# The end block of a key band and the short chunk of w_down as half-array products, one behind the other

## The chip, the core and the metric

The kernel runs on one core of a Trainium2 chip. The metric is the device time of one execution in microseconds (us), as a median over runs. Five engines share the work: TensorE (matrix products; PE in the profile, its weight loads are PEld), VectorE (DVE), ScalarE (ACT), GpSimd (POOL), and SyncE (SP), which issues most DMAs. A product of TensorE has a stationary operand, which is loaded first, and a moving operand, whose columns are streamed past it. Both have the contraction on the 128 partitions. The sum goes to PSUM, in banks.

## The reference

One transformer block with two halves, on X of 8 sequences, 2048 positions and 256 features, all in float32:

```
def layer(x):
    x = x + attention(layernorm(x))
    return x + ffn(layernorm(x))

def attention(X):                       # D[n, m] = 0.9 ** |n - m|
    Q, K, V = xpos(X @ W_Q), xpos(X @ W_K, downscale=True), X @ W_V
    p = softmax(Q @ K.T) * D            # the decay comes after the softmax
    return p @ V

def ffn(x):                             # fq: blocks of 16 along the last axis,
    gate = fq(x) @ fq(w_gate).T         # rounded to 4-bit floats and scaled back
    y = fq(x) @ fq(w_up).T              # w_gate, w_up: (704, 256)
    return fq(silu(gate) * y) @ fq(w_down).T    # w_down: (256, 704)
```

All scores are needed for the softmax's maximum and sum. In the product with V, however, a key that is 833 positions away has the weight 0.9^833, about 8e-39, which is below float32's normal range.

## The kernel before, in words

The 16,384 positions are 128 blocks of 128 rows, numbered n; i = n % 16 is a block's place in its sequence. The program is written by hand in its order, step by step: `step(n)` (from L842) emits the work of a software pipeline on all five engines. For block n it computes the scores (`scores`, two halves of 1024 keys), their maxima (`maximum`, VectorE, L543) and the exponentials (ScalarE). For block n-1 it does the decays, the product with V, the residual and the second normalization; for n-2 the gate and up products; for n-3 the rounding of the hidden values, mostly on VectorE and GpSimd; for n-5 the down product and the output. Each engine runs its instructions in the order in which they are emitted. Waits are semaphores that are derived from the tiles that an instruction reads and writes. Only the last steps (from `z = total - 1` on) are written out separately.

**The band.** `band(n)` is the list of key blocks from i-7 to i+7 that exist (BAND = 7): 8 blocks at a sequence's ends, up to 14 or 15 in its middle. `turn_p` turns the exponentials so that keys lie on the partitions (transposes on VectorE within 32x32 squares, L261, and a DMA there and back). `decays` (L621) multiplies them by the decay table into the tile p_t, on VectorE, in pieces of up to four blocks in key order. `attend` (L636) then runs one product for each key block, in key order, into the PSUM tile o: p_t's block is stationary, the block of V moving (L644). Within the band's outermost blocks only half the keys are within 833 positions. For the two middle blocks of a sequence (i = 7 and 8, `whole`), whose bands have an outermost block at both ends, `join_values` puts the two useful halves of V into one tile, so that one product does for both ends. All other blocks have one such end: i+7, the last in key order, for i up to 6; i-7, the first, for i from 9 on. It is taken with all 128 partitions.

**The short chunk.** The 704 hidden features are FC = 6 chunks for `down` (L768): 640 are five whole chunks, 64 are left. The sixth chunk takes features 576 to 703, so that it has 128 rows; the first 64 of them were in the fifth chunk already, and the rows of `wd_t` (w_down turned) that they meet are set to zero (L163). `turn_h` (L743) turns h in two pieces, 640 and the last 128 features; `keep_h` copies the result to `h_t`. The six products of `down` go into the PSUM tile d.

**The order around the change.** On TensorE a step is: scores of block n, a projection in most steps, `down(n-5)`, `attend(n-1)`, then gate and up of n-2. On VectorE, between the second maximum and the rounding of h stands `decays(n-1)`.

Every float32 product is a pair of weight loads and a pair of passes in the profile. o and d have PSUM buffers of their own (pool `ps_m`, two buffers).

Of the kernel before, what the change touches and what calls it, by code (L numbers as in the profile page):

```python
# [9 lines left out]
F32 = mybir.dt.float32  # L10
# [5 lines left out]
P = 128  # L16
GROUP = 512
BPG = GROUP // P
# [3 lines left out]
BAND = 7  # L22
SQ = 32
NSQ = P // SQ
# [10 lines left out]
def preln_xpos_retention_fp4_ffn_kernel(  # L35
# [13 lines left out]
    nc = tc.nc  # L49
    B, L, H = x.shape  # L50
    F = w_gate.shape[0]
    HC = H // P
    NB = L // P
    NG = L // GROUP
    FH = F // 2
    FC = -(-F // P)
# [8 lines left out]
    ps_m = ctx.enter_context(tc.tile_pool(name="ps_m", bufs=2, space=bass.MemoryType.PSUM))  # L65
# [58 lines left out]
    ident = cpool.tile([P, P], F32, name="ident")  # L124
# [35 lines left out]
    wg_t = cpool.tile([P, HC, F], F32, name="wg_t")  # L160
    wu_t = cpool.tile([P, HC, F], F32, name="wu_t")
    wd_t = cpool.tile([P, FC, H], F32, name="wd_t")
    nc.gpsimd.memset(wd_t[: FC * P - F, FC - 1, :], 0.0)  # L163


    def layernorm_scale(mv, n, name):
# [82 lines left out]

    def turn(dst, pieces, name, tag):


        n = sum(src.shape[-1] for src in pieces) // NSQ
        sq = prob_p.tile([P, dst.shape[-1]], F32, tag=tag, bufs=1, name=f"sq_{name}")
        sq = sq[:, : NSQ * n].rearrange("p (c f) -> p c f", c=NSQ)
        at = 0
        for src in pieces:
            w = src.shape[-1] // NSQ  # L260
            nc.vector.transpose(  # L261
                sq[:, :, at : at + w].rearrange("p c (k i) -> p k c i", i=SQ),
                src.rearrange("p (k c i) -> p k c i", c=NSQ, i=SQ),
            )
            at += w
        there = dram.tile([NSQ, SQ, NSQ, n], F32, tag=f"turn_{n}", name=f"there_{name}")
        nc.scalar.dma_start(there.rearrange("a i c f -> (a i) c f"), sq)
        dst = dst[:, : NSQ * n].rearrange("p (a f) -> p a f", a=NSQ)
        for c in range(NSQ):
            nc.sync.dma_start(dst[ts(c, SQ)], there[:, :, c, :].rearrange("a i f -> i a f"))  # L270
# [5 lines left out]

    LAST = (FC - 1) * P - (F - P)

# [4 lines left out]
    weight_rows, weight_fp4, scratch = {}, {}, {}  # L287

    def hold_ffn_weights():
        for name in "gu":  # L290
            weight_rows[name] = act_p.tile(
                [P, FULL - 1, H], F32, tag="kt", bufs=2 * NG, name=f"w{name}_rows"
            )
        whole = act_p.tile([P, 2 * GROUP], F32, tag="kt", bufs=2 * NG, name="wgu_rows")
        weight_rows["r"] = whole[:, : 3 * H].rearrange("p (c k) -> p c k", c=3)
        scratch["r"] = whole[:, 3 * H :]
        big = act_p.tile([P, 2 * GROUP], F32, tag="kt", bufs=2 * NG, name="wbig")
        for c in range(HC):
            whole = act_p.tile([P, BPG * H], F32, tag="vt", bufs=6, name=f"wd_rows{c}")
            weight_rows["d", c] = whole[:, :F]  # L300
            scratch["gu"[c]] = whole[:, F:]
        for key in "gur":
            raw = weight_rows[key].rearrange("p c k -> p (c k)")
            weight_fp4[key] = Fp4(raw, P, raw.shape[-1], f"w{key}", big, scratch[key])
        for c in range(HC):
            weight_fp4["d", c] = Fp4(weight_rows["d", c], P, F, f"wd{c}", big)

    def load_ffn_weights(key):
        if key in ("g", "u"):
            src = {"g": w_gate, "u": w_up}[key]  # L310
            nc.sync.dma_start(
                weight_rows[key], src[: (FULL - 1) * P, :].rearrange("(c p) k -> p c k", p=P)
            )
        elif key == "r":
            raw = weight_rows[key]
            for c, src in enumerate((w_gate, w_up)):
                nc.sync.dma_start(raw[:, c, :], src[(FULL - 1) * P : FULL * P, :])
                nc.sync.dma_start(raw[c * REST : (c + 1) * REST, 2, :], src[FULL * P :, :])
        else:
            nc.sync.dma_start(weight_rows[key], w_down[ts(key[1], P), :])  # L320

    def turn_ffn_weights(key):
        raw = weight_rows.pop(key)
        if key[0] == "d":
            cols, per = ts(key[1], P), FC // 2
            for first in range(0, FC, per):
                pt = ps_m.tile([P, per, P], F32, tag="m", name=f"pt_wd_{first}")
                for fc in range(first, first + per):
                    at = min(fc * P, F - P)
                    nc.tensor.transpose(pt[:, fc - first, :], raw[:, at : at + P], ident)  # L330
                whole = min(per, FC - 1 - first)
                nc.scalar.copy(wd_t[:, first : first + whole, cols], pt[:, :whole, :])
                if whole < per:
                    nc.scalar.copy(wd_t[LAST:, FC - 1, cols], pt[LAST:, per - 1, :])
            return
        n = raw.shape[1]
        if key == "r":
            pts = []
            for hc in range(HC):
                pt = ps_m.tile([P, n, P], F32, tag="m", name=f"pt_wr_{hc}")  # L340
                for c in range(n):
                    nc.tensor.transpose(pt[:, c, :], raw[:, c, ts(hc, P)], ident)
                pts.append(pt)
            for c, dst in enumerate((wg_t, wu_t)):
                for hc, pt in enumerate(pts):
                    nc.scalar.copy(dst[:, hc, (FULL - 1) * P : FULL * P], pt[:, c, :])
                    nc.scalar.copy(dst[:, hc, FULL * P :], pt[:, 2, c * REST : (c + 1) * REST])
            return
        pt = ps_s.tile([P, 2 * GROUP], F32, tag="s", name=f"pt_w{key[0]}")
        pt = pt[:, : HC * n * P].rearrange("p (h c r) -> p h c r", h=HC, c=n)  # L350
        for hc in range(HC):
            for c in range(n):
                nc.tensor.transpose(pt[:, hc, c, :], raw[:, c, ts(hc, P)], ident)
        dst = {"g": wg_t, "u": wu_t}[key]
        nc.scalar.copy(dst[:, :, : n * P].rearrange("p h (c r) -> p h c r", c=n), pt)
# [36 lines left out]
    qt, kt, vt = {}, {}, {}  # L392
# [127 lines left out]
    total = B * NB  # L520
# [74 lines left out]
    def band(n):  # L595
        return [k for half in range(2) for k in keys_of(n, half)]
# [3 lines left out]
    ends_of = {}  # L600

    def whole(n):
        return BAND <= n % NB < NB - BAND
# [32 lines left out]
    def attend(n):  # L636
        b, i = divmod(n, NB)
        po = ps_m.tile([P, H], F32, tag="m", name=f"o_{n}")
        keys, p_t = band(n), turned.pop(n)
        values = [(j, vt[b, k // BPG][:, k % BPG, :]) for j, k in enumerate(keys)]  # L640
        if whole(n):
            values = values[1:-1] + [(0, ends_of.pop(n))]
        for j, v in values:
            nc.tensor.matmul(  # L644
                po, p_t[:, j, :], v, start=(j == values[0][0]), stop=(j == values[-1][0])
            )
        attended[n] = po

    def inverse_sum(n):
# [93 lines left out]
    def turn_h(n):  # L743
        h = hid[n][1]
        if n >= total - 4:
            pt = ps_s.tile([P, FC + 2, P], F32, tag="s", name=f"pt_h_{n}")[:, :FC, :]
            at_once = FC // 2 if n == total - 1 else FC
            for f in range(0, FC, at_once):
                for fc in range(f, f + at_once):
                    at = min(fc * P, F - P)  # L750
                    nc.tensor.transpose(pt[:, fc, :], h[:, at : at + P], ident)
                chunks = slice(f, f + at_once)
                keep_h(n, pt.rearrange("p c (a i) -> p c a i", a=NSQ)[:, chunks], chunks)
        else:
            turn(h, [h[:, : (FC - 1) * P], h[:, F - P : F]], f"h{n}", "sq_h")

    def keep_h(n, src=None, chunks=slice(0, FC)):
        x1, h, h_t = hid[n]
        if chunks.start == 0:
            h_t = ffn_p.tile([P, FC, P], F32, tag="h_t", name=f"h_t_{n}")  # L760
        nc.scalar.copy(  # L761
            h_t[:, chunks].rearrange("p c (a i) -> p c a i", a=NSQ),
            in_runs(h) if src is None else src,
        )
        hid[n] = (x1, h, h_t)


    def down(n):  # L768
        x1, _, h_t = hid.pop(n)
        pd = ps_m.tile([P, H], F32, tag="m", name=f"d_{n}")  # L770
        pairs = [(h_t[:, fc, :], wd_t[:, fc, :]) for fc in range(FC)]
        if z - 5 < n < z:
            pairs.insert(0, (ident, x1))
        for j, (lhs, rhs) in enumerate(pairs):
            nc.tensor.matmul(pd, lhs, rhs, start=(j == 0), stop=(j == len(pairs) - 1))  # L775
        hid[n] = (x1, pd)
# [16 lines left out]
    pairs = [range(c, c + 2) for c in range(0, BPG, 2)]  # L793
# [236 lines left out]
    half = FC // 2 * P // QBLK  # L1030
# [60 lines left out]
```

## Time and profile before

| | |
|---|---|
| median of 3 runs | 2833.9 us (2833.09 to 2834.87) |
| the profiled execution's own time | 2833.93 us |
| its span in the profile | 2832.1 us |
| granted clock of TensorE | 0.998 |
| busy: TensorE, loads | 2809.3 us, 1842.3 us |
| busy: VectorE, GpSimd, ScalarE | 2476.0, 1412.8, 1078.0 us |
| a step, in the middle of the run | 19.4 to 23.7 us |

Times in the profile are counted from the span's start. A group's row gives source line, engine, operation, the tiles written and read (out<-in), the form, how often, then the busy time in us and the mean length of one in ns, then the idle time of the engine just before them and who ended it. A row of the timeline gives start and length in us, engine, line, operation, tiles, form and how many instructions were merged into it, with idle time before it in brackets. Matmul records are longer than the distance from one to the next, since they overlap.

### The profile page before, as it was taken

What the parts mean: (1) busy time and instruction counts of PE and PEld (TensorE: products, weight loads), DVE (VectorE), ACT (ScalarE), POOL (GpSimd) and SP (SyncE); (2) the same over time, 40 slices, a digit from 0 to 9 for tenths busy, and PEclk for the clock granted to TensorE, in tenths of its full rate; (3) what the DMA queues carried; (4) which work ended last, traced back from release to release, by engine and by line L of the source; (5) the groups of instructions that cost most, each with busy time, mean ns of one, the idle gap of its engine ahead of it and who ended that gap; (6) DMA issues with size and microseconds to landing.
All of it is one profiled execution on the core that took longest, in us unless ns stands there. A gap on an engine that the chain in (4) does not pass through costs nothing.

```text
span 2832.1 us, 34344 instructions
## 1 busy us (share of the span) xinstructions
PE 2809.3 (99%) x9754; PEld 1842.3 (65%) x9754; DVE 2476.0 (87%) x5665; ACT 1078.0 (38%) x1707; POOL 1412.8 (50%) x1328
## 2 busy tenths in 40 slices
PE   9899999999999999999999999999999999999999
PEld 6566666666666666666666666666666666666666
DVE  8988888988888888898888888888888888888888
ACT  4333334333433443333334333433343343333332
POOL 6554455444555445544555544554545445545443
PEclk9999999999999999999999999999999999999999
DMA  5355544555455555555544555455545554445541
GB/s 192 115 169 171 170 142 147 176 180 155 142 162 170 166 159 155 154 161 171 161 152 152 167 174 161 145 168 167 167 145 160 166 167 148 143 123 160 150 152 50
DMA packets 364320, 441.45 MB, mean 156 GB/s; under 512 B 101600, under 2 KB 311648, under 8 KB 364128
## 3 DMA queue, kind: packets, MB, share of 16 engines
q1 hardware_dynamic: 306096, 263.58, 34.5%
q10 hardware_dynamic: 58032, 175.66, 16.3%
q8 instruction: 77, 1.26, 0.2%
q14 instruction: 115, 0.94, 0.1%
HBM read 246.68 MB, written 192.41 MB: 155 GB/s over the span
## 4 chain that ended last, share of the span: by engine, by line
PE 88%; DVE 5%; POOL 1%; ACT 1%; issue 1%; DMA 1%; SPq 0%; DVEq 0%; ACTq 0%; POOLq 0%
PE s L531 28%; PE o L644 21%; PE d L775 10%; PE gate L710 10%; PE up L710 10%; PE pp_q L467 3%; PE pp_k L467 3%; PE pv L505 3%; DVE m L543 1%; DVE p_t L614 0%; DMA there_p<-sq_p 0%; DVE h L739 0%; DVE amax_h L192 0%; POOL h L239 0%; POOL h L240 0%
## 5 line engine op out<-in xcount | busy, mean ns | idle before, releaser
L531 PE MATMUL s<-kt,qt 128*128 128x512 f32 x2048 | 900.7, 592 | 2.2 <-DVE rot_q L487 2.0
L531 PEld LDWEIGHTS s<-kt,qt 128*128 128x128 f32 x2048 | 388.3, 190 | 459.5 <-issue 420.1
L644 PE MATMUL o<-v,p_t 128*128 128x256 f32 x2880 | 646.6, 381 | 8.1 <-DVE p_t L614 8.1
L644 PEld LDWEIGHTS o<-v,p_t 128*128 128x128 f32 x2880 | 548.2, 191 | 88.2 <-issue 7.6
L564 ACT ACT_TABLE_LOAD x125 | 160.4, 1283 | 981.7 <-DVE nmax L548 970.8
L239 POOL TENSOR_TENSOR h<-h,big_h 128x704 f32<-128x704 f32 x125 | 211.2, 1690 | 525.5 <-DVE big_h L234 521.5
L733 ACT ACT_TABLE_LOAD x126 | 161.7, 1283 | 604.3 <-DVE xq L671 296.7
L775 PE MATMUL d<-wd_t,h_t 128*128 128x256 f32 x1536 | 352.6, 379 | 1.0 <-ACT h_t L761 1.0
L543 DVE TENSOR_REDUCE m<-s 128x1 f32<-128x1024 f32 x256 | 309.2, 1208 | 32.6 <-PE s L531 32.1
L775 PEld LDWEIGHTS d<-wd_t,h_t 128*128 128x128 f32 x1536 | 291.6, 190 | 69.9 <-issue 28.9
L710 PE MATMUL gate<-wg_t,xq_t 128*128 128x352 f32 x1024 | 324.5, 459 | 0.9 <-ACT xq_t L696 0.9
L710 PE MATMUL up<-wu_t,xq_t 128*128 128x352 f32 x1024 | 324.0, 459 | 0.0
L564 ACT ACTIVATE p<-s,nmax 128x1024 f32<-128x1024 f32 x256 | 283.0, 1111 | 24.0 <-DVE nmax L548 16.8
L206 POOL TENSOR_TENSOR h<-h,inv_h 128x704 f32<-128x704 f32 x126 | 174.7, 1387 | 208.2 <-DVE inv_h L204 157.0
L710 PEld LDWEIGHTS up<-wu_t,xq_t 128*128 128x128 f32 x1024 | 194.4, 190 | 107.9
L206 POOL TENSOR_TENSOR xq<-xq,inv_x 128x256 f32<-128x256 f32 x127 | 79.0, 622 | 357.5 <-DVE inv_x L204 315.6
L710 PEld LDWEIGHTS gate<-wg_t,xq_t 128*128 128x128 f32 x1024 | 193.8, 190 | 90.6 <-ACT xq_t L696 2.5
L614 DVE TENSOR_TENSOR p_t<-runs,decay_sb 128x512 f32<-128x512 f32 (+1 forms) x446 | 244.1, 600 | 4.0 <-issue 0.4
L261 DVE STREAM_TRANSPOSE sq_p<-p 128x1024 f32<-128x1024 f32 (+7 forms) x239 | 224.0, 973 | 3.4 <-ACT p L564 3.4
L240 POOL TENSOR_TENSOR h<-h,big_h 128x704 f32<-128x704 f32 x125 | 210.3, 1682 | 9.8
L239 POOL TENSOR_TENSOR xq<-xq,big_x 128x256 f32<-128x256 f32 x127 | 93.3, 735 | 199.8 <-DVE big_x L234 199.8
L243 POOL TENSOR_TENSOR h<-h,scale_h 128x704 f32<-128x704 f32 x126 | 174.9, 1388 | 17.4 <-DVE h L240 7.6
(166 smaller groups left out, 3475.9 us busy)
## 6 DMA issues: line engine op xcount, KB each, us to landing
there_h<-sq_h ACTq DMA_DIRECT2D x124, 384.0 KB, 4.6
h<-there_h SPq DMA_DIRECT2D x496, 96.0 KB, 2.2
rope_k<-in_rope_dram SPq DMA_DIRECT2D x32, 512.0 KB, 6.1
rope_q<-in_rope_dram SPq DMA_DIRECT2D x32, 512.0 KB, 5.7
xr<-in_L_attn_X_dram SPq DMA_DIRECT2D x128, 128.0 KB, 2.2
out_dram<-x SPq DMA_DIRECT2D x128, 128.0 KB, 5.3
x<-in_L_attn_X_dram SPq DMA_DIRECT2D x31, 512.0 KB, 4.2
there_xq<-sq_xq ACTq DMA_DIRECT2D x124, 128.0 KB, 1.7
```

Source lines behind the costliest of these rows:

```text
L206: (on or self.wide_on).tensor_tensor(self.v3, self.v3, self.wide(inv), ALU.mult)
L239: self.wide_on.tensor_tensor(v, v, big, ALU.add)
L240: self.wide_on.tensor_tensor(v, v, big, ALU.subtract)
L243: (last_on or self.wide_on).tensor_tensor(self.v3[:, k], self.v3[:, k], wide[:, k], ALU.mult)
L261: nc.vector.transpose(sq[:, :, at : at + w].rearrange("p c (k i) -> p k c i", i=SQ), src.rearrange("p (k c i) -> p k c i", c=NSQ, i=SQ),)
L531: nc.tensor.matmul(ps[:, j, :], q[:, dc, ts(i % BPG, P)], kt[b, half * 2 + j][:, dc, :], start=(dc == 0), stop=(dc == 1),)
L543: nc.vector.tensor_reduce(raw_scores[n][:, half : half + 1], raw_scores[n, half], AX.XY, ALU.max)
L564: nc.scalar.activation(pr, raw_scores.pop((n, half)).rearrange("p j k -> p (j k)"), AF.Exp, bias=nmax, accum_out=sums[:, half : half + 1],)
L614: nc.vector.tensor_tensor(p_t[rows, at : at + w, :].rearrange("p k (a i) -> p k a i", a=NSQ), pt[rows, of : of + w], decay_sb[rows, d + BA ...
L644: nc.tensor.matmul(po, p_t[:, j, :], v, start=(j == values[0][0]), stop=(j == values[-1][0]))
L710: nc.tensor.matmul(pss[which][:, half, :FH], xq_t[:, hc, :], (wg_t, wu_t)[which][:, hc, ts(half, FH)], start=(hc == 0), stop=(hc == HC - 1),)
L775: nc.tensor.matmul(pd, lhs, rhs, start=(j == 0), stop=(j == len(pairs) - 1))
```

## The change

The end block of the 14 blocks of a sequence that have one end takes 64 partitions, the half with the useful keys: the lower half (partitions 0 to 63) of block i+7, or the upper half of block i-7. It becomes the first product of `attend`. The short chunk of `down`, which stays the last product there, takes 64 partitions too, on the half that the following `attend` does not use: `short_chunk(n)` looks at block n+4, whose `attend` comes directly after `down(n)`. The last 64 features therefore have to lie on the upper half for some blocks and on the lower for others. `wd_t` holds them in both halves, instead of zeros in one. For `h_t`, `turn` gets an option `exchange`, which transposes the last 128 features in two pieces that change places. The number of products stays the same.

```
-    nc.gpsimd.memset(wd_t[: FC * P - F, FC - 1, :], 0.0)
...
-    def turn(dst, pieces, name, tag):
+    def turn(dst, pieces, name, tag, exchange=False):
         n = sum(src.shape[-1] for src in pieces) // NSQ
+        if exchange:
+            pieces, last = pieces[:-1], pieces[-1]
...
+        if exchange:
+            for c, half in ((0, slice(P // 2, P)), (NSQ // 2, slice(0, P // 2))):
+                nc.vector.transpose(
+                    sq[:, c : c + NSQ // 2, at : at + SQ].rearrange("p c (k i) -> p k c i", i=SQ),
+                    last[:, half].rearrange("p (k c i) -> p k c i", c=NSQ // 2, i=SQ),
+                )
...
-    LAST = (FC - 1) * P - (F - P)
+    UPPER, LOWER = slice(P // 2, P), slice(0, P // 2)
+    def end_of(n):
+        i = n % NB
+        if i < BAND:
+            return i + BAND, LOWER
+        if i >= NB - BAND:
+            return i - BAND, UPPER
+        return None, None
+    def short_chunk(n):
+        return LOWER if n + 5 < total and end_of(n + 4)[1] == UPPER else UPPER
...
     def turn_ffn_weights(key):
...
-            for first in range(0, FC, per):
-                pt = ps_m.tile([P, per, P], F32, tag="m", name=f"pt_wd_{first}")
-                for fc in range(first, first + per):
-                    at = min(fc * P, F - P)
-                    nc.tensor.transpose(pt[:, fc - first, :], raw[:, at : at + P], ident)
-                whole = min(per, FC - 1 - first)
-                nc.scalar.copy(wd_t[:, first : first + whole, cols], pt[:, :whole, :])
-                if whole < per:
-                    nc.scalar.copy(wd_t[LAST:, FC - 1, cols], pt[LAST:, per - 1, :])
+            at = [min(fc * P, F - P) for fc in range(FC)] + [(FC - 1) * P]
+            for first in (0, per):
+                chunks = at[first:] if first else at[:per]
+                pt = ps_m.tile([P, len(chunks), P], F32, tag="m", name=f"pt_wd_{first}")
+                for j, c in enumerate(chunks):
+                    nc.tensor.transpose(pt[:, j, :], raw[:, c : c + P], ident)
+                full = min(per, FC - 1 - first)
+                nc.scalar.copy(wd_t[:, first : first + full, cols], pt[:, :full, :])
+                if first:
+                    nc.scalar.copy(wd_t[UPPER, FC - 1, cols], pt[UPPER, full, :])
+                    nc.scalar.copy(wd_t[LOWER, FC - 1, cols], pt[LOWER, full + 1, :])
...
     def attend(n):
...
-        values = [(j, vt[b, k // BPG][:, k % BPG, :]) for j, k in enumerate(keys)]
+        end, rows = end_of(n)
+        pairs = []
+        for j, k in enumerate(keys):
+            v = vt[b, k // BPG]
+            if k == end:
+                pairs.insert(0, (p_t[rows, j, :], v[rows, k % BPG, :]))
+            else:
+                pairs.append((p_t[:, j, :], v[:, k % BPG, :]))
         if whole(n):
-            values = values[1:-1] + [(0, ends_of.pop(n))]
-        for j, v in values:
-            nc.tensor.matmul(
-                po, p_t[:, j, :], v, start=(j == values[0][0]), stop=(j == values[-1][0])
-            )
+            pairs = pairs[1:-1] + [(p_t[:, 0, :], ends_of.pop(n))]
+        for j, (lhs, rhs) in enumerate(pairs):
+            nc.tensor.matmul(po, lhs, rhs, start=(j == 0), stop=(j == len(pairs) - 1))
...
     def turn_h(n):
...
-            turn(h, [h[:, : (FC - 1) * P], h[:, F - P : F]], f"h{n}", "sq_h")
+            pieces = [h[:, : (FC - 1) * P], h[:, F - P : F]]
+            turn(h, pieces, f"h{n}", "sq_h", exchange=short_chunk(n) == LOWER)
...
     def down(n):
...
-        pairs = [(h_t[:, fc, :], wd_t[:, fc, :]) for fc in range(FC)]
+        pairs = [(h_t[:, fc, :], wd_t[:, fc, :]) for fc in range(FC - 1)]
+        rows = short_chunk(n)
+        pairs.append((h_t[rows, FC - 1, :], wd_t[rows, FC - 1, :]))
```

The rows of w_down are held in a tile that is wider than its 704 columns, so that the set-up can transpose columns 640 to 767 of it; what lies beyond 704 isn't used.

More of the change, by code (lines that the diff above doesn't have):

```diff
@@ L299, in hold_ffn_weights @@
             whole = act_p.tile([P, BPG * H], F32, tag="vt", bufs=6, name=f"wd_rows{c}")
-            weight_rows["d", c] = whole[:, :F]
+            weight_rows["d", c] = whole
             scratch["gu"[c]] = whole[:, F:]
@@ L319, in load_ffn_weights @@
         else:
-            nc.sync.dma_start(weight_rows[key], w_down[ts(key[1], P), :])
+            nc.sync.dma_start(weight_rows[key][:, :F], w_down[ts(key[1], P), :])
     def turn_ffn_weights(key):
```

## The prediction

> **What bounds the kernel now.** I read the page's busy times first, then its groups, then the timeline around the place that the change touches.
>
> ```profile
> PE 2809.3 (99%) x9754; PEld 1842.3 (65%) x9754; DVE 2476.0 (87%) x5665; ACT 1078.0 (38%) x1707; POOL 1412.8 (50%) x1328
> L644 PE MATMUL o<-v,p_t 128*128 128x256 f32 x2880 | 646.6, 381 | 8.1 <-DVE p_t L614 8.1
> L775 PE MATMUL d<-wd_t,h_t 128*128 128x256 f32 x1536 | 352.6, 379 | 1.0 <-ACT h_t L761 1.0
> L543 DVE TENSOR_REDUCE m<-s 128x1 f32<-128x1024 f32 x256 | 309.2, 1208 | 32.6 <-PE s L531 32.1
> ```
>
> TensorE is idle for 23 of 2832 us, so any pass taken away can be worth its time and any new wait costs its length. Each float32 matmul is two passes (768 products d, 1536 records). VectorE is second, and it waits for the scores (32.1 us): it is tied to TensorE's pace.
>
> ```profile
> 1015.34 0.38 PE L775 MATMUL d<-wd_t,h_t 128*128 128x256 f32 x1
> 1015.56 0.38 PE L644 MATMUL o<-v,p_t 128*128 128x256 f32 x1
> 1015.56 0.19 PEld L644 LDWEIGHTS o<-v,p_t 128*128 128x128 f32 x1
> ...
> 2545.64 0.19 PEld L644 LDWEIGHTS o<-v,p_t 128*128 128x128 f32 x1 [0.93 <-DVE p_t L614]
> 2545.64 0.48 PE L644 MATMUL o<-v,p_t 128*128 128x256 f32 x1 [0.53 <-DVE p_t L614]
> ...
> 2545.64 0.30 PEld L644 LDWEIGHTS o<-v,p_t 128*128 128x128 f32 x2 [0.93 <-DVE p_t L614]
> ```
>
> The last pass of down and the first of attend start 0.216 us apart. That is a pass of 256 columns (the 12 of d between 1012.97 and 1015.56 give the same). A record lasts 0.38, so 0.163 of it is a tail under the next pass. The load of the next weights starts as a pass starts. The stalled start (block 114) shows a load by itself: the matmul's record is 0.48 instead of 0.38, and the two loads together last 0.30 where one lasts 0.19; so a load holds its successor for about 0.106, and a matmul streams that long after its load has begun.
>
> The next view is where the two halves will meet: block 80 (the first of its sequence), 84 (its fifth), 117 (in the last sequence). Each time, the first line is attend's weights being made by decays, the second attend.
>
> ```profile
> 1814.11 1.29 DVE L614 TENSOR_TENSOR p_t<-runs,decay_sb 128x512 f32<-128x512 f32 x2
> 1815.06 0.81 PE L644 MATMUL o<-v,p_t 128*128 128x256 f32 x3
> ...
> 1897.58 1.89 DVE L614 TENSOR_TENSOR p_t<-runs,decay_sb 128x512 f32<-128x512 f32 x3
> 1898.57 1.24 PE L644 MATMUL o<-v,p_t 128*128 128x256 f32 x5
> ...
> 2601.21 1.19 DVE L543 TENSOR_REDUCE m<-s 128x1 f32<-128x1024 f32 x1
> 2602.61 2.10 DVE L614 TENSOR_TENSOR p_t<-runs,decay_sb 128x512 f32<-128x512 f32 x4
> 2603.46 2.11 PE L644 MATMUL o<-v,p_t 128*128 128x256 f32 x9
> ```
>
> The pieces end at 1815.40, 1899.47 and 2604.71; attend starts at 1815.06, 1898.57 and 2603.46. So attend runs 0.35, 0.90 and 1.25 us ahead of its last piece, and may, because it takes the blocks in key order.
>
> **The change, part by part.**
>
> *The halves side by side: a gain.* A half-array product still streams 256 columns twice, so by itself it costs the same two passes. Down's last (A) and attend's first (B) are passes A1 A2 B1 B2. Matmuls start in program order in every record of the trace, and A1/A2 and B1/B2 use the same half. So only B1 can run beside A2: at most one pass of four, 0.216 us. The least is 0 (no side by side at all). Nothing in this trace is half-array, so the value has to come from the nearest row, the load. There a load starts when the matmul before it in program order starts; B1's load then starts with A2, holds 0.106, and B1 streams 0.108 after A2: gain 0.108 a pair. I take that; the ends 0 and 0.216 stay.
>
> Pairs: down(n-5) stands directly ahead of attend(n-1) in steps 5 to 126, for blocks 4 to 125. These are 122, less the 16 middle blocks (two in each sequence) whose ends were joined before: 106.
>
> The Trainium skill (TensorE: Matmul & The Clock Gate, Part 3) says that a load for another row group is pulled ahead of matmuls in flight and that matmuls of different row groups start some 4 ns apart. By it the pair gains a whole pass, and the sum is that of the first rival below; no row here shows it.
>
> *The end block first: a loss.* For blocks 0 to 6 of a sequence the end block is i+7, the last in the band, whose weights are in the last piece of decays. Put first, attend's first matmul waits for that piece, and the remaining products, gate and up, and the next block's scores queue behind it; VectorE's next maxima wait for those. For blocks 9 to 15 the end is the first block: no new wait. A wait costs the lateness plus 0.16 (in block 114 p_t ends 0.05 before the load starts, and 0.106 for the load). I read the lateness in the same way for every block:
> - Sequences 2 to 7, first block: 0.35, 0.36, 0.35, 0.37, 0.35, 0.36, sum 2.14, with 6 x 0.16 it is 3.1.
> - The same, fifth block: 0.90, 0.30, 1.15, 0.93, 0.90, 1.15, sum 5.33, with 0.96 it is 6.3. If VectorE is not delayed along, what the first block has lost counts here too, and only 3.2 is new.
> - The other early blocks of these six start 0.1 to 2.5 after their last piece: nothing.
> - Last sequence, blocks 113 to 118: 0.54, 0.88, 1.02, 1.15, 1.25, 1.28, sum 6.12, with 0.96 and less 0.1 for four that stall already: 6.7. There the wait comes back each step, because m<-s starts at 2601.21, just as the scores end: TensorE late makes the pieces late.
> - First sequence: blocks 3 and 4 wait 3.7 and 2.7 us for p_t anyway, and attend stalls inside as well. 0 to 0.7.
>
> Together 13.0 to 16.8; I take 15.
>
> *What the wait swallows.* Where attend waits for VectorE, a TensorE that came earlier only waits longer. That takes the pairs of blocks 0 to 4 in six sequences and of the last sequence's first 7: 37. The other 69 keep their gain: 69 x 0.108 = 7.5 (ends: 0, and 69 x 0.216 = 14.9).
>
> *Into and out of the half-array form.* 106 pairs and 28 halves alone make 134 stretches, 268 changes of form. The nearest rows are the seams between unlike work: transposes beside float32 products and 256 beside 352 or 512 columns all follow at their usual 0.109, 0.216, 0.295 or 0.429 us, so 0. The far end is the tail of a record, 0.163. I take 0; the tail is a rival. The Trainium skill (TensorEngine Tiling (Array Packing), Key Properties) speaks against it: changing the tiling mode, not just the tile, drains TensorE. If that means a tail, its sum is the second rival's upper end. No seam here changes the form, so the rows don't contradict it.
>
> *The exchange (55 blocks).* One 128x128 transpose of h (269 ns) becomes two of 128x64. Rows of 286, 420 and 554 ns for 128, 256 and 384 columns give about 220 each: 0.17 more, 9 us of VectorE in all. They fall in the steps that attend to blocks 7 to 13, where attend starts 0.1 (once) to 3.7 us after its first piece, mostly over 1. Only in the last sequence is that room 0.26. Cover gone, six times 0.17 is 1.0; I take 0.3.
>
> *Set-up.* Two more transposes (0.109), two more ScalarE copies (0.26), one GpSimd memset less (0.31), in steps 4 and 5, where attend waits 2.7 us for VectorE: 0 to 0.7, I take 0.2.
>
> Sum, from the profiled execution's own 2833.93 (its span is 2832.1; the median of the three is 2833.9, the same): 2833.93 + 15 - 7.5 + 0 + 0.5 = 2841.9.
>
> **The rivals.**
> - *A whole pass a pair, and no price for the form.* 15 - 14.9 + 0.5: 2834.5, no change. For it: with 0.106 a load, both A2's and B1's fit under A1. Against: no load in the trace starts ahead of a matmul that has not begun.
> - *Each change of form empties the array.* 231 changes that no wait covers (268 less 37) at 0.163 are 37.7; on the first rival that is 2872, at half a tail 2853. For it: the two forms could lead sums out differently; against: the seamless seams.
> - *The halves run one behind the other.* No gain: 2833.9 + 15.5 = 2849.
> - *Faster.* VectorE's slack lets it run on while TensorE waits, so that nothing is swallowed: 106 x 0.216 = 22.9 against 13.0 and 0.5 gives 2824.5. For it: VectorE is 13% idle. Against: the 32.1 us that it waits for scores, and the last sequence. It decides once a pair is worth over 0.18 us in the end (13.5 + 5.7, over 106).
>
> **How the numbers follow.** A measurement of this kernel can tell 0.2%, 5.7 us, from no change. Forecast 0.33, the first rival 0.22, emptying 0.25, one behind the other 0.05, faster 0.15. The forecast case alone reaches from 2836 to 2850 (gains of 0.05 to 0.15 a pair, waits of 13.0 to 16.8); a quarter of it is within 0.2%. The first rival, being near the middle, gives 0.03 to slower and 0.01 to faster. Slower: 0.25 + 0.25 + 0.05 + 0.03 = 0.58; same 0.08 + 0.18 = 0.26; faster 0.15 + 0.01 = 0.16. The range leaves out the lower part of the faster case and the worst of emptying: 2826 to 2871.
>
> **What would show it.** In block 117, attend's first matmul starts only after p_t's four pieces, with some 1.3 us of idle time ahead of it; waits of o for p_t rise from 8.1 to some 20 us. In a pair, B1 starts 0.108 after A2 (0.00 for the first rival, 0.216 or more if one behind the other). The spacing from the last whole pass to A1, and from B2 to the next whole pass, is 0.216; 0.38 means that the array emptied. VectorE's busy time rises by 9 us. I am wrong if p_t's last piece arrives earlier, or if half-array passes are not 0.216 us.

## The result and the profile after

The changed kernel takes 2857.9 us as a median of six runs (2853.2 to 2859.8), against 2833.4 for the kernel before (2831.7 to 2834.9): a ratio of 1.0082, with a 95% interval of 1.0072 to 1.0092. That is 24.5 us slower, where 8.0 were forecast. The profiled execution took 2859.16 us, with a span of 2857.3.

The page and the groups of the changed kernel, in the lines that answer to those shown of before:

```profile
PE 2828.5 (99%) x9756; PEld 1789.0 (63%) x9756; DVE 2472.9 (87%) x5720; ACT 1078.3 (38%) x1709; POOL 1413.7 (49%) x1327
L674 PE MATMUL o<-v,p_t 128*128 128x256 f32 (+1 forms) x2880 | 679.9, 388 | 14.3 <-DVE p_t L637 13.6
L806 PE MATMUL d<-wd_t,h_t 128*128 128x256 f32 (+1 forms) x1536 | 377.5, 387 | 1.0 <-ACT h_t L790 1.0
L566 DVE TENSOR_REDUCE m<-s 128x1 f32<-128x1024 f32 x256 | 309.8, 1210 | 44.2 <-PE s L554 43.7
```

Two things grew. The idle time of TensorE ahead of attend went from 8.1 to 14.3 us; that is the wait for p_t's last piece, but only 6 us of it. The rest of the loss is counted as busy: attend's product group went from 646.6 to 679.9, down's from 352.6 to 377.5, with the same number of records. (TensorE's busy time as a whole grew by 19.2 only, from 2809.3 to 2828.5: where the two halves run at the same time, their records are counted in both groups.) Kept apart by form:

```profile
L806 PE MATMUL d<-wd_t,h_t 128*128 128x256 f32 x1280 | 297.4, 379 | 1.0 <-ACT h_t L790 1.0
L806 PE MATMUL d<-wd_t,h_t 64*128 64x256 f32 x256 | 89.1, 428 | 0.0
L674 PE MATMUL o<-v,p_t 64*128 64x256 f32 x224 | 78.4, 430 | 14.3 <-DVE p_t L637 13.6
```

A half-array record of down occupies 0.348 us (89.1 over 256), a whole one 0.232 (297.4 over 1280). VectorE now waits longer for the scores (43.7 instead of 32.1), since TensorE comes later with them.

### One pair, pass by pass

The timeline of the changed kernel at block 43, where down and attend meet; the rows are from narrow stretches, so that most hold one instruction (the first two are down's last whole passes):

```profile
1022.59 0.38 PE L806 MATMUL d<-wd_t,h_t 128*128 128x256 f32 x1
1022.80 0.38 PE L806 MATMUL d<-wd_t,h_t 128*128 128x256 f32 x1
1023.11 0.18 PEld L806 LDWEIGHTS d<-wd_t,h_t 64*128 64x128 f32 x1 [0.33 <-issue]
1023.12 0.18 PEld L674 LDWEIGHTS o<-v,p_t 64*128 64x128 f32 x1
1023.11 0.48 PE L806 MATMUL d<-wd_t,h_t 64*128 64x256 f32 x1
1023.12 0.48 PE L674 MATMUL o<-v,p_t 64*128 64x256 f32 x1
1023.43 0.38 PE L806 MATMUL d<-wd_t,h_t 64*128 64x256 f32 x1
1023.44 0.38 PE L674 MATMUL o<-v,p_t 64*128 64x256 f32 x1
1023.74 0.19 PEld L674 LDWEIGHTS o<-v,p_t 128*128 128x128 f32 x1 [0.33 <-issue]
```

This shows the two prices of the change.

*Side by side.* The order is A1 B1 A2 B2, not A1 A2 B1 B2. Attend's first pass starts 6 ns after down's (1023.113 and 1023.119 in the records), before down's second. Both passes of both halves overlap, so four passes take the time of two: 0.432 us less.

*Into the half-array form and out of it.* Between whole passes, a load starts as the pass before it starts. Here the load of the new form starts 0.307 after the last whole pass has started, where the next pass would have come after 0.216. So TensorE first lets 0.091 more pass, and then the load's 0.106 lies open too (the matmul's record is 0.48 long, as after a stall): 0.197 in all. Out of the form it is 0.194. Both figures are the same, within some 0.002, at nearly every stretch that doesn't wait; five stretches of down alone near the end, with transposes behind them, cost 0.147 to leave.

So a stretch of half-array work costs 0.391, and a pair that runs side by side saves 0.432, of which the 6 ns take a little: counted from the last whole pass before it to the first whole pass behind it that isn't stalled, such a pair is 0.034 us shorter than four whole passes would be. 81 of the pairs that run side by side have this figure; four in the last sequence (blocks 121 to 124) cost 0.09.

### Where pairs break up

Of the 134 stretches in the trace, 85 have this form (d o d o, after the tiles that the passes write). 22 hold down alone, 16 of them at 0.391 and five at 0.344 (the last ends the program's products), and 6 attend alone, at 0.391 or, where it waits, more. In the other 21 the order is d d o o, as at block 116, in the same kernel's timeline:

```profile
2600.11 1.89 DVE L637 TENSOR_TENSOR p_t<-runs,decay_sb 128x512 f32<-128x512 f32 x3
2600.73 0.29 PEld L806 LDWEIGHTS d<-wd_t,h_t 64*128 64x128 f32 x2 [0.33 <-issue]
2602.06 0.29 PEld L674 LDWEIGHTS o<-v,p_t 64*128 64x128 f32 x2 [1.04 <-DVE p_t L637]
2602.06 1.11 PE L674 MATMUL o<-v,p_t 64*128 64x256 f32 x3 [0.64 <-DVE p_t L637]
2602.69 0.30 PEld L674 LDWEIGHTS o<-v,p_t 128*128 128x128 f32 x2 [0.33 <-issue]
```

p_t's last piece ends at 2602.00. Down's two halves have been through by then, attend's come afterwards. Such a stretch pays for the change of form, waits, and gains nothing: 0.67 to 0.79 us net at ten of the twelve in sequences 2 to 7 (1.1 and 1.7 at the other two), and up to 2.0 in the last sequence. 18 of the 21 are the first and fifth blocks of sequences 2 to 7 and blocks 113 to 118, the very blocks whose lateness the prediction had added up; the others are 4, 12 and 125.

### The profile page after: what moved, and what is told of

Same layout as the page of the kernel before. It is cut to its first block, busy times and chain, and to the rows that moved or that the text cites. A ratio compares the mean times of both kernels' runs of the same rounds, so it can differ in the third digit from the quotient of the medians.

```text
span 2857.3 us, 34404 instructions
## 1 busy us (share of the span) xinstructions
PE 2828.5 (99%) x9756; PEld 1789.0 (63%) x9756; DVE 2472.9 (87%) x5720; ACT 1078.3 (38%) x1709; POOL 1413.7 (49%) x1327
## 3 DMA queue, kind: packets, MB, share of 16 engines
q10 hardware_dynamic: 58032, 175.66, 16.2%
## 4 chain that ended last, share of the span: by engine, by line
PE 77%; DVE 4%; ACT 2%; DMA 1%; issue 1%; POOL 0%; SPq 0%; ACTq 0%; DVEq 0%; POOLq 0%
PE s L554 24%; PE o L674 18%; PE d L806 9%; PE gate L738 9%; PE up L738 9%; PE pp_q L490 3%; PE pp_k L490 3%; PE pv L528 2%; DVE m L566 1%; DVE p_t L637 1%; DMA there_p<-sq_p 1%; ACT p L587 1%; ACT x L447 0%; DVE h L767 0%; ACT L587 0%
## 5 line engine op out<-in xcount | busy, mean ns | idle before, releaser
L674 PE MATMUL o<-v,p_t 128*128 128x256 f32 (+1 forms) x2880 | 679.9, 388 | 14.3 <-DVE p_t L637 13.6
L674 PEld LDWEIGHTS o<-v,p_t 128*128 128x128 f32 (+1 forms) x2880 | 528.6, 190 | 130.6 <-issue 40.4
L806 PE MATMUL d<-wd_t,h_t 128*128 128x256 f32 (+1 forms) x1536 | 377.5, 387 | 1.0 <-ACT h_t L790 1.0
L566 DVE TENSOR_REDUCE m<-s 128x1 f32<-128x1024 f32 x256 | 309.8, 1210 | 44.2 <-PE s L554 43.7
L806 PEld LDWEIGHTS d<-wd_t,h_t 128*128 128x128 f32 (+1 forms) x1536 | 280.6, 189 | 105.7 <-issue 71.9
L587 ACT ACTIVATE p<-s,nmax 128x1024 f32<-128x1024 f32 x256 | 283.0, 1110 | 27.2 <-DVE nmax L571 19.2
```

The source lines that it names most:

```text
L566: nc.vector.tensor_reduce(raw_scores[n][:, half : half + 1], raw_scores[n, half], AX.XY, ALU.max)
L587: nc.scalar.activation(pr, raw_scores.pop((n, half)).rearrange("p j k -> p (j k)"), AF.Exp, bias=nmax, accum_out=sums[:, half : half + 1],)
L674: nc.tensor.matmul(po, lhs, rhs, start=(j == 0), stop=(j == len(pairs) - 1))
```

## The experiments

The theory after reading this trace: a stretch of half-array work costs 0.39, a pair saves 0.43 if both halves are ready, and the wait for p_t's last piece both costs time and breaks pairs up. The rivals: the wait alone makes the loss; the change of form alone makes it; a pair is worth a pass at most, as the prediction had it. All times are medians, beside runs of the kernel before on the same chip: 2835.3 us for the first four, 2835.2 for the last two.

### The order alone

```
-        for j, v in values:
+        elif n % NB < BAND:
+            values = values[-1:] + values[:-1]
+        for j, v in values:
```

> The kernel before, with one edit: for blocks 0 to 6 of a sequence the end block's product comes first in attend, still with all 128 partitions. No half-array product anywhere. The theory read from the changed kernel's trace (a stretch of half-array work costs 0.39 us to enter and leave, a pair that runs side by side saves 0.43, and attend's wait for its last piece of p_t comes on top) and the prediction agree here: a loss of 10 to 17 us, 2843 to 2850, with attend in the last sequence starting behind its last piece. Rival (the wait is absorbed and the whole 24.5 us of the change come from the change of form): no more than 3 us, below 2837.

Measured: 2845.95 us, +10.6, ratio 1.0037 (1.0024 to 1.0050). TensorE's waits for p_t in the list of waits (us in total, how many, the longest), of the kernel before and then with the order alone:

```profile
PE o L644 <- DVE p_t L614: 8.1, 5, 3.7
```

```profile
PE o L646 <- DVE p_t L614: 18.2, 22, 4.9
```

And the timeline with the order alone, at block 117:

```profile
2610.16 2.10 DVE L614 TENSOR_TENSOR p_t<-runs,decay_sb 128x512 f32<-128x512 f32 x4
2612.32 0.48 PE L646 MATMUL o<-v,p_t 128*128 128x256 f32 x1 [1.04 <-DVE p_t L614]
```

Seventeen more waits, 10.1 us more. At block 117, attend starts 0.06 after the end of all four pieces, not 1.25 ahead of it. The wait is real, and it is less than half of the change's loss. By the starts of each block's scores in the two traces, blocks 15 to 111 lose 5.1 us and blocks 111 to 127 another 5.2.

### The last piece made first

```
-        for c in range(first, last, BPG):
+        pieces = list(range(first, last, BPG))
+        if n % NB < BAND:
+            pieces = pieces[-1:] + pieces[:-1]
+        for c in pieces:
```

> The changed kernel, with one edit: for blocks 0 to 6 decays makes the piece that holds the end block first and the others behind it in their order. The wait for the last piece is gone, and nothing else. Theory: in the changed kernel 18 pairs in the second to last sequences were broken up by that wait at a net cost of some 0.7 to 2 us each instead of -0.03; about 17 us go, 2841, and nearly all 106 pairs show the order d o d o. What stays over before is 22 stretches of down alone at 0.39 (8.6), a few of attend alone (2) and 106 pairs at -0.03 (-3.6): some 7 us. Rival (the change of form alone makes the loss): 2855 or more. Rival (the wait alone makes it): 2834.

Measured: 2843.66 us, +8.4 (ratio 1.0031, 1.0019 to 1.0043). 98 pairs now run as d o d o, 8 are still broken up. In the timeline, block 117 is whole again:

```profile
2612.23 0.18 PEld L677 LDWEIGHTS o<-v,p_t 64*128 64x128 f32 x1
2612.24 0.48 PE L677 MATMUL o<-v,p_t 64*128 64x256 f32 x1
2612.55 0.38 PE L809 MATMUL d<-wd_t,h_t 64*128 64x256 f32 x1
```

Against the changed kernel (+23.4 on its chip, see the last experiment) this is 15.1 us better. The wait's 10.6 and 13 pairs that run side by side again (13 x 0.432 = 5.6) would make 16.2. Counted stretch by stretch in the two traces, waits included, the 106 pairs cost 19.4 us in the changed kernel and 4.9 here, 14.5 less. (The two traces' spans lie only 12.5 apart, because the profiled execution here, 2846.59 us, is the slowest of its six.) Neither rival holds: the wait is not all, and the form is not all.

### Both on the same half

```
-        return LOWER if n + 5 < total and end_of(n + 4)[1] == UPPER else UPPER
+        return LOWER if n + 5 < total and end_of(n + 4)[1] == LOWER else UPPER
```

> The changed kernel, with one edit: down's short chunk takes the same half as the end block that follows it, so that nothing can run side by side. Theory: the 85 pairs that ran side by side lose 0.432 each, 36.7 us, the 21 that the wait broke up lose nothing: 2858 + 37 = 2895. Prediction's figure of 0.108 a pair: 2867. A whole pass a pair (0.216), the most that the prediction allowed: 2876.

Measured: 2888.86 us, +53.5 (ratio 1.0185, 1.0168 to 1.0202). The 106 pairs are all d d o o, one pass after the other at 0.216, as in the timeline at block 43:

```profile
1031.44 0.29 PEld L806 LDWEIGHTS d<-wd_t,h_t 64*128 64x128 f32 x2 [0.33 <-issue]
1031.77 0.40 PEld L674 LDWEIGHTS o<-v,p_t 64*128 64x128 f32 x2
1031.98 1.22 PE L674 MATMUL o<-v,p_t 64*128 64x256 f32 x4
```

Nothing opens between down's passes and attend's here: changing the product within the form costs nothing. 96 of the 106 stretches cost 0.39; the other ten wait as well. Against the changed kernel it is 30.1 us slower, less than the 36.7 expected. The difference is found in the broken pairs: from block 15 to 111 the two traces drift apart by 26.9 us. The 72 unbroken pairs there are worth 72 x 0.425 = 30.6. Of the 12 broken ones, nine fall to 0.39, since TensorE now comes late enough for the last piece, and three stay about as they were; together they cost 3.4 less. 30.6 - 3.4 = 27.2. So a pair is worth some 0.43; 0.216 would have given 18, 0.108 only 9.

### The short chunk alone

```
-        pairs = [(h_t[:, fc, :], wd_t[:, fc, :]) for fc in range(FC)]
+        pairs = [(h_t[:, fc, :], wd_t[:, fc, :]) for fc in range(FC - 1)]
+        pairs.append((h_t[P // 2 :, FC - 1, :], wd_t[P // 2 :, FC - 1, :]))
```

> The kernel before, with one edit: down's sixth chunk takes 64 partitions (the upper half), and attend stays as it was. So 128 times a half-array product stands alone between whole-array products and nothing is gained. Theory: 0.39 us each, of which 0.197 to enter and 0.194 to leave, 50 us: 2883. Rival (only the tail of a record, 0.163, is lost at each change of form): 42 us, 2875. Rival (the form costs nothing, as the prediction took it): 2833.

Measured: 2877.35 us, +42.0 (ratio 1.0147, 1.0132 to 1.0163). By the time alone the rival with the tail, 2875, would have been right. The trace decides otherwise: all but a few of the 128 stretches cost 0.391 (120 exactly so). The timeline at block 43:

```profile
1026.64 1.65 PE L776 MATMUL d<-wd_t,h_t 128*128 128x256 f32 x6
1027.60 0.29 PEld L776 LDWEIGHTS d<-wd_t,h_t 64*128 64x128 f32 x2 [0.33 <-issue]
1028.22 0.73 PEld L644 LDWEIGHTS o<-v,p_t 128*128 128x128 f32 x4 [0.33 <-DVE h L230]
```

The last whole pass starts at 1027.29 and the half-array load 0.31 later, and the next whole load 0.30 after the last half-array pass. That is the way in and out of the changed kernel's trace; a tail alone, 0.163 at each change, would be less. (The "DVE h" that the last row names had ended 0.27 before; it is no cause.) What the total lacks is given back where TensorE waited for VectorE before: at block 8 the kernel is 1.1 us ahead of the kernel before, although three stretches lie behind it, and blocks 111 to 119 lose 1.8 instead of 3.1. From block 15 to 111, where TensorE sets the pace, 96 stretches cost 35.4 us, 0.37 each (37.5 at 0.391).

### Pairs and nothing else

On top of the last piece made first, in its main lines:

```
+        if not 4 <= n <= total - 3:
+            return None, None
...
-        return LOWER if n + 5 < total and end_of(n + 4)[1] == UPPER else UPPER
+        rows = end_of(n + 4)[1]
+        return slice(0, P) if rows is None else LOWER if rows == UPPER else UPPER
...
+        if short_chunk(n) == slice(0, P):
+            nc.gpsimd.memset(h[:, F : FC * P], 0.0)
...
-            pieces = [h[:, : (FC - 1) * P], h[:, F - P : F]]
+            short = slice(F - P, F) if short_chunk(n) != slice(0, P) else slice((FC - 1) * P, FC * P)
+            pieces = [h[:, : (FC - 1) * P], h[:, short]]
```

> The kernel with the last piece first, and half-array products only where a pair stands: for the blocks whose down has no partner (the 16 middle blocks' partners and the last ones) the sixth chunk takes 128 partitions again, with zeros written by GpSimd into the unused 64 features, and the attends without a partner take their end block whole and in key order. 28 stretches fewer. Theory: of the 8.4 us that the kernel with the last piece first was over the kernel before, 22 x 0.39 = 8.6 and some 2 of the single attends go; 106 pairs at -0.034 are left, less a few that VectorE still breaks up. That gives 0 to 3 us under the kernel before, at most 0.1%: no version that beats it clearly. Rival (the loss does not go by stretches but with VectorE's pieces or the exchange): it stays 5 us or more above.

Measured: 2835.35 us against 2835.15, ratio 1.0001 (0.9992 to 1.0010): the same. In the groups by form, the half-array records of down and attend are equal now, 106 pairs of two passes each:

```profile
L815 PE MATMUL d<-wd_t,h_t 64*128 64x256 f32 x212 | 73.8, 428 | 0.0
L680 PE MATMUL o<-v,p_t 64*128 64x256 f32 x212 | 73.7, 428 | 2.6 <-DVE p_t L640 2.5
```

The 8.4 us have gone with the 28 stretches that had no partner. 99 pairs run side by side: 87 are 0.034 shorter than four whole passes, the others mostly 0.07 to 0.19 longer, 1.7 us of gain in all. Seven broken pairs cost 5.9 by the trace, of which 3.1 is one in the first sequence, where the kernel before waits too. So this use of half the array is worth nothing here even where every half has a partner. No version of it that would beat the kernel before was found.

### The changed kernel again

The kernel of the change, without an edit.

> The changed kernel as it is, beside the kernel with pairs alone on the same chip: 2856 to 2860 by the first measurement, 0.8% over the kernel before. If the difference between the changed kernel and the others came from the chip, it would be elsewhere.

Measured: 2858.6 us, +23.4, ratio 1.0082 (1.0069 to 1.0096), as at first; the stretches are 85, 21, 22 and 6 again. With the others this gives the account of the change: 15.1 us for the wait and the pairs that it breaks up, 8.15 for stretches without a partner, and 0.2 for the pairs, which can't be told from none (the interval of the experiment with pairs alone is 2.3 us less to 2.8 more).

## Why the prediction was right and where it was not

**The direction and the range** held, and the mechanism of the wait. The size did not: 24.5 us where 8.0 were summed. Two steps were wrong in opposite directions, and for an unbroken pair they nearly cancel (0.432 saved, 0.391 paid, where 0.108 and 0 were taken). That 2857.9 lies within the range is owed in part to this and to the rival that emptied the array, which held the upper end open; it isn't owed to the sum.

**"At most one pass of four, 0.216 us"** failed. The step took the order of the passes, A1 A2 B1 B2, for the order of starting. The trace before could only show passes of one form, 128 by 128. In the changed kernel both first passes start within 6 ns, and 0.432 is saved, twice the bound and four times the 0.108 that was taken. The Trainium skill's sentence on it (TensorE: Matmul & The Clock Gate, Part 3: loads for another row group pulled ahead, matmuls some 4 ns apart) agrees with this trace: attend's first load starts before down's second (1023.12 and 1023.22), and the matmuls 6 ns apart.

**"Into and out of the half-array form: I take 0"** failed. The seams of the trace before all lay within one form, so they were no near rows for this. The measured price is 0.197 in and 0.194 out; even the far end, a tail of 0.163, was too low, because the load starts 0.091 late and then lies open: 0.091 + 0.106. The sign that was named for it, a spacing of 0.216 or else 0.38, read 0.31, which is neither. The 0.106 had been read in the stalled start of block 114 and used for the pairs, but not here. The Trainium skill (TensorEngine Tiling (Array Packing), Key Properties) says that a change of the tiling mode, not of the tile, drains TensorE. The trace agrees with both halves: 0.39 a stretch for the change of form, and no such price between down's half and attend's other half (6 ns).

**The wait, 15 us (13.0 to 16.8)**: the mechanism was right, the size too large. Alone it measured 10.6: 5.1 for blocks 15 to 111 (6.3 to 9.4 were summed) and 5.2 for the last 16 blocks (6.7). In the middle sequences the low reading was the right kind: at block 84, the fifth of its sequence and 0.90 late, the wait came to 0.60 with the load, not to the 1.06 of the high reading; the difference is about the first block's wait (0.50 at block 80). That a wait takes the pair's gain with it was foreseen, at 0.108; it takes 0.43, and the price of the form stays.

**"What the wait swallows": 37 pairs.** 21 were broken up, 18 of them where the waits had been read. The 37 also counted blocks 1 to 3 of six sequences, whose gain would only lengthen the fifth block's wait; those pairs do run side by side. How much of their gain is lost at the next wait wasn't measured.

**The halves alone, 28 stretches**, were counted and priced at 0. They are the 8 us that were left once the wait was gone: 22 of down alone at 0.391 would be 8.6, and what the six of attend alone, in the first four blocks and the last two, cost in the end wasn't separated. The rival in which each change of form empties the array was the nearest case, 2853 to 2872, though partly by luck: it had a change at no more than 0.163 (0.197 and 0.194 were measured) and a pair's gain at 0.216 (0.432).

**The exchange** was put at 9 us of VectorE's time, with cover. It is 3.3 by the busy times: 18.6 + 18.1 us for the pieces of 128 and 64 columns, where all the pieces of 128 took 33.4 before; the small ones take 202 ns and overlap. VectorE's whole busy time even fell by 3 us, so that sign would have misled.

## What to carry to other kernels

Half-array products have to win back the price of their stretch: here a stretch costs 0.39 us and one pair of 256 float32 columns saves 0.43. A half without a partner loses the 0.39, nearly a whole product's time (0.432). By these figures a second pair in the same stretch would be the first real gain; that is an estimate, and no run here has one. Count the stretches and the halves alone before the pairs. When a product is moved to the front of an accumulation, look up which piece of its operand is made last; making that piece first took away 15 of 24 us.

## What the runs showed that was not expected

- The order of the passes of two products is not the same in every pair. Where attend's weights are ready, its first pass goes ahead of down's second (0.314 earlier at block 43); where they are late, down's second goes first (block 116). So the program alone doesn't fix it. Why the hardware takes the one order or the other wasn't tested beyond that.
- A change between whole-array and half-array work costs 0.197 and 0.194 us, the same at nearly every stretch; 0.091 of the way in passes before the load starts, and 0.106 is the load. The split of the way out was not measured by itself.
- A change of product within the form costs nothing: passes on the same half follow each other at 0.216.
